# Turning normalised activations with 16-bit DMA transposes instead of TensorE, with the order of all stages written anew

## The chip, the cores and the metric

The kernel runs on one core of a Trainium2 chip. The metric is the device time of one execution in microseconds (us), and the time of a kernel is the median of its runs. One execution is also profiled; spans, waits and durations below come from that one.

## What is computed

Two graph layers run one after the other on 128 graphs of 128 nodes with 256 features, in fp32. The adjacency entries are 0 or 1. Cut to what matters:

```python
# layer 0: attention with one value matrix per adjacency value, then a feed-forward net
q, k = src @ Wq + bq, src @ Wk + bk                       # 8 heads of 32
attn = softmax(q k^T / sqrt(32))
out  = sum over r of (attn * (adj == r)) @ (src @ Wv[r] + bv[r])
x = LN(src + out @ Wo + bo) * g1 + beta1                  # norm 0
y = LN(x + gelu(x @ W1 + b1) @ W2 + b2) * g2 + beta2      # norm 1
# layer 1: two graph-attention steps, then a feed-forward net
h = gat(gat(y, adj, W1, a1), adj, W2, a2)                 # softmax over axis 1, masked by adj
z = LN(y + h) * g_ln1 + b_ln1                             # norm 2
out = LN(z + relu(z @ w_ff1 + b_ff1) @ w_ff2 + b_ff2) * g_ln2 + b_ln2   # norm 3
```

LN subtracts the mean of a row of 256 and divides by the root of its variance plus 1e-5.

## The kernel before, in words

The 16384 tokens are worked in 32 groups of 512 (four graphs, `G = 4`, `T = 512`). A group has its tokens in two layouts. In token layout a tile is 128 tokens on partitions x 4 blocks x 256 features (`S["x"]`, the residual, normalised in place). In feature layout it is 128 features x 2 halves x 512 tokens (`yT`), which TensorE needs as an operand. `transposed` (L293 to L306) goes from the first to the second: eight TensorE transposes into two PSUM banks (L300), and two ScalarE activations (L303) that take the result out of PSUM and apply the norm's gain and offset, which are per-partition columns in that layout.

A norm i of a group goes through these steps. `added` or the end of `ffn` adds to `x` and takes row statistics with VectorE (`variances`, L320 and L322). `root` (L334, L335) makes 1/sqrt(var + eps), a VectorE instruction and a power on GpSimd. `normed` (L338 to L357) makes (x - mean) / std: for norms 0 to 2 four ScalarE activations (L349) with a small VectorE one ahead (L344), for norm 3 four VectorE ones (L354). `turned` calls `transposed` and, for norms 0 and 2, makes four sums and differences `yS` on VectorE (L389 to L392). `scaled` (L367) multiplies the token-layout tile by the gain and adds the offset, in two VectorE passes of two 128x512 instructions each; its result is the residual of what follows.

The matrix products of the feed-forward nets and of the q, k, v projections use a scheme with seven instead of eight half-size products, so that sums such as `yS` stand ahead of them and VectorE adds (L466, L470, L479 to L481, L503 to L524) behind. `ffn` (L394 to L528) is a generator with 22 steps: 14 of the first layer, each one product of two 128x256 matmul instructions (L411) into the PSUM banks `fa`, `fe` or `seeded`, with ScalarE copies `p7` (L456) and `p16` (L460) and activations (L435); and 8 of the second layer, seven of them with a product of eight 128x128 instructions (L420). An fp32 matmul shows as two in the trace. `first_ffn` is layer 0's net and `second_ffn` layer 1's. `projected` makes q, k and v (L641); `attention` makes scores (L709), exponentials (L717), masked copies (L727), sums and denominators (L744, L758), reciprocals (L775, L777), and the output projection (L793); `layer1` makes both graph-attention steps. In these `spread` sends a 2 KB row block to HBM and back, broadcast over partitions (L840, L841). Of exp and gelu each needs its own ScalarE function table, loaded by `table` (L537).

The engines run their instructions in the order in which the kernel issues them (`manual_schedule`); nothing rearranges them later. That order is written by hand: every stage is a generator that stops at `yield`, and `in_order` takes steps of several groups by turns. In the steady part, a pass of the loop over `g` works on the first net of group g+1, the graph layer and second net of g, the attention and projections of g+2 and g+3, and the last norm of g-1. All DMAs of the steady part are issued by SyncE (SP), in order: `entered` loads a group's xT, adj and x together, and `store` writes a finished group.

In code, the part that the change replaces first:

```python
for b in range(G):
    nc.tensor.transpose(
        pt[:, b * P : (b + 1) * P], y[:, b, c * P : (c + 1) * P], k.ident
    )
nc.scalar.activation(
    yT[:, c, :], pt, AF.Identity, bias=bc[:, c : c + 1], scale=gc[:, c : c + 1]
)
```

Of the kernel before, what the change touches and what calls it, by code (L numbers as in the profile page):

```python
# [11 lines left out]
I32 = mybir.dt.int32  # L12
AF = mybir.ActivationFunctionType
# [12 lines left out]
G = 4  # L26
# [4 lines left out]
class Weights:  # L31
# [16 lines left out]
    def col(self, name):  # L48
        v = self.a[name]
        t = self.tile([P, v.shape[0] // P], "c_" + name)  # L50
        with self.nc.allow_non_contiguous_dma(reason="a bias vector as columns"):
            self.queue.dma_start(t, v.rearrange("(c p) -> p c", p=P))
        return t
# [45 lines left out]

def over(r, n=G):  # L100
    return r[:, None, :].to_broadcast([P, n, r.shape[1]])
# [6 lines left out]
def fast_pass(ctx, tc, a, out):  # L108
# [17 lines left out]
    io = ctx.enter_context(tc.tile_pool(name="io", bufs=4))  # L126
# [29 lines left out]
    def entered(g):  # L156

        xt = load_xT(g)
        ad, xr = load_rest(g)
        return dict(xt=xt, ad=ad, x=xr, g=g, direct={NG - 1: 0, NG - 2: 1}.get(g, 2))  # L160
# [44 lines left out]
    b0 = k.tile([P, NCH], "b0")  # L205
# [11 lines left out]
    g1c, be1c = k.col("L0_gnn_g1"), k.col("L0_gnn_beta1")  # L217
    w1, b1 = forms("L0_gnn_W1"), k.col("L0_gnn_b1")
    g1r = k.row("L0_gnn_g1")
# [15 lines left out]
    g2c, be2c = k.col("L0_gnn_g2"), k.col("L0_gnn_beta2")  # L235
    g2r, be2r = k.row("L0_gnn_g2"), k.row("L0_gnn_beta2")
    u1, c1 = forms("L1_gnn_w_ff1"), k.col("L1_gnn_b_ff1")
    u2 = forms("L1_gnn_w_ff2")
    h1c, he1c = k.col("L1_gnn_g_ln1"), k.col("L1_gnn_b_ln1")
# [9 lines left out]
    wu = k.tile([P, NCH, NU], "wu")  # L249

# [43 lines left out]
    def transposed(y, gc, bc, n):  # L294

        yT = w2p.tile([P, NCH, T], F32, tag="yT", name="yT_" + n)
        for c in range(NCH):
            pt = ps_s.tile([P, T], F32, tag="s", name=f"pt_{n}_{c}")
            for b in range(G):
                nc.tensor.transpose(  # L300
                    pt[:, b * P : (b + 1) * P], y[:, b, c * P : (c + 1) * P], k.ident
                )
            nc.scalar.activation(  # L303
                yT[:, c, :], pt, AF.Identity, bias=bc[:, c : c + 1], scale=gc[:, c : c + 1]
            )
        return yT  # L306

# [3 lines left out]
    def variances(S, i, bs):  # L311
# [9 lines left out]
        for b in range(bs.start, bs.stop):  # L321
            nc.vector.bn_aggr(S["mv", i][:, b, :], st[:, b % 2, :])  # L322

    def added(S, i, p, po):

        x = flat(S["x"][:, pair(p), :])
        nc.vector.tensor_add(x, po, x)
        variances(S, i, pair(p))

    def root(S, i, bs=slice(0, G)):  # L330

        n = f"{i}_{S['g']}_{bs.start}"
# [4 lines left out]
    def normed(S, i, bs=slice(0, G)):  # L337


        x, mv, rs = S["x"], S["mv", i], S["rs", i]  # L340
        scalar = i < 3 or bs.stop - bs.start < G
        if scalar:
            sh = small.tile([P, G], F32, tag="sh", name=f"sh_{i}_{S['g']}_{bs.start}")
            nc.vector.scalar_tensor_tensor(  # L344
                sh[:, bs], mv[:, bs, 0], -1.0, rs[:, bs], op0=ALU.mult, op1=ALU.mult
            )
        for b in range(bs.start, bs.stop):
            if scalar:
                nc.scalar.activation(  # L349
                    x[:, b, :], x[:, b, :], AF.Identity, bias=sh[:, b : b + 1],  # L350
                    scale=rs[:, b : b + 1],
                )
            else:
                nc.vector.tensor_scalar(  # L354
                    x[:, b, :], x[:, b, :], mv[:, b, 0:1], rs[:, b : b + 1],
                    op0=ALU.subtract, op1=ALU.mult,
                )  # L357
# [3 lines left out]
    cols = {0: (g1c, be1c), 1: (g2c, be2c), 2: (h1c, he1c)}  # L361

    def scaled(S, i, step, ps=range(G // 2)):
        for p in ps:
            x = S["x"][:, pair(p)]
            op = (nc.vector.tensor_mul, nc.vector.tensor_add)[step]
            op(x, x, over(rows[i][step], 2))  # L367

    def norm(S, i):

        root(S, i)
        yield
        normed(S, i)
        yield
        for step in range(2):
            scaled(S, i, step)
            yield

    TH = T // 2

    def turned(S, i):
        n = f"{i}_{S['g']}"
        S["xT", i + 1] = yT = transposed(S["x"], *cols[i], n)
# [8 lines left out]
        nc.vector.tensor_sub(ys[:, 3], a12, ys[:, 1])  # L392

    def ffn(S, i, wa, ba, func, wb_):  # L394
# [91 lines left out]
        def quarter(q, k2):  # L486

            return x[:, pair(q), k2 * P : (k2 + 1) * P]
# [52 lines left out]
    def in_order(*steps):  # L541


        for s in steps:
            if callable(s):
                s()
                continue
            gen, n = s if isinstance(s, tuple) else (s, 1)
            for _ in range(n):
                next(gen, None)  # L550

    def prepared(S):
        g, xr, ad = S["g"], S["x"], S["ad"]
        for p in range(G // 2):
            nc.vector.tensor_add(xr[:, pair(p)], xr[:, pair(p)], over(bo, 2))

# [6 lines left out]
    def projections(S):  # L563

# [9 lines left out]
        for h, (o, bias) in enumerate((("qT", bq), ("kT", bk))):  # L574
            S[o] = w1p.tile([P, NCH, T], F32, tag=o, name=f"{o}_{n}")
            for m in range(NCH):
# [6 lines left out]
                nc.scalar.activation(S[o][:, m, :], pq, AF.Identity, bias=bias[:, m : m + 1])  # L583
                yield
        S["v"] = v = w1p.tile([P, G, 2 * D], F32, tag="v", name="v_" + n)
        for b in range(G):
# [8 lines left out]
            nc.vector.tensor_add(v[:, b, D:], pv[:, D:], bv)  # L595
            yield
# [3 lines left out]
    def projected(S):  # L600
# [15 lines left out]
        S["qT"], S["kT"] = qk  # L616
        S["v"] = v = w1p.tile([P, G, 2 * D], F32, tag="v", name="v_" + n)

        for values in range(2):
# [26 lines left out]
            def result(k2, h):  # L646

                if values:
# [44 lines left out]
    def scores(S, p):  # L693

        qT, kT = S["qT"], S["kT"]
# [36 lines left out]
    def sums(S, p):  # L732


        e, pm = S["e", p], S["pm", p]
# [174 lines left out]
    def store(S, bs=slice(0, G)):  # L910
        t0 = S["g"] * T
# [27 lines left out]
    with tc.manual_schedule(engines={ET.PE, ET.Activation, ET.DVE, ET.SP, ET.Pool}):  # L939
# [4 lines left out]
        none = iter(())  # L944
        st = [first, second] + [None] * (NG - 2)
        S1 = st[1]
        gwu, pr, at = graph_weights(), projections(first), attention(first)
        pr1, at1 = projections(S1), attention(S1)
        n0, n1_, n0_ = norm(first, 0), norm(first, 1), norm(S1, 0)

        def output_bias():
# [7 lines left out]
            prepared(first)  # L959

        in_order(
            (pr, 4), (at, 3), (pr, 2), (at, 5), (pr, 2), at, output_bias, pr1, (at, 3), pr1, at, n0, (pr1, 3), (at1, 2), n0,
            lambda: combined(w1), pr1, at1, lambda: turned(first, 0), (at1, 4),
        )
        f1 = first_ffn(first)
        prepared(S1)
        st[2] = entered(2)
        pr = projected(st[2])
        in_order(
            gelu, (f1, 2), at1, at1, pr1, pr1, (f1, 4), at1, f1, f1, n0, lambda: combined(w2), f1,  # L970
            f1, n0, f1,
            (f1, 3), gwu, at1, f1, gwu, f1, at1, gwu,
            f1, at1, f1, gwu, lambda: combined(wqk), at1, f1, n0_, pr, n0_, (f1, 4), n1_, (pr, 5), lambda: turned(S1, 0),
        )
        for g in range(NG - 1):
            S, S1 = st[g], st[g + 1]
            more = g + 2 < NG
            f1, f2 = first_ffn(S1), second_ffn(S)
            n1, n2 = norm(S1, 1), norm(S, 2)
            at = n0 = none  # L980
            if more:
                S2 = st[g + 2]
                at, n0 = attention(S2), norm(S2, 0)
            ahead = lambda: turned(S, 2)
# [399 lines left out]
```

## Time and profile before

| | |
|---|---|
| runs | 2741.42, 2742.82, 2742.77 us; median 2742.77 |
| span of the profiled execution | 2740.1 us |
| TensorE busy | 2705.4 us (99%), 21621 matmuls |
| VectorE busy | 2282.8 us (83%) |
| ScalarE busy | 1610.6 us (59%) |
| GpSimd busy | 135.6 us (5%) |
| DMA | 86.12 MB, mean 31 GB/s |

The profiled execution's own time is not listed apart from its span; the median lies 2.7 us above that span, and what lies around the span is taken from this. PE in the profile is TensorE's matmuls, PEld its weight loads, DVE is VectorE, ACT ScalarE, POOL GpSimd, SP SyncE. A group's row gives the line, engine, operation, the tiles out and in, their shapes and the count; then its busy time in us, the mean ns of one, and how long the engine stood idle just before, with what ended that wait. The matmuls overlap one another: their mean duration is longer than the distance from one's start to the next one's, and that distance is what one costs in a full queue. The same holds, less strongly, for DVE and ACT. The granted TensorE clock is 1.00 in all windows read but the last 20 us.

### The profile page before, as it was taken

To read this page: it belongs to the slowest core of one execution; us is meant where nothing else is said; L and a number is where in the kernel's file an instruction comes from. 1 tells how busy PE (TensorE), PEld (TensorE's weight loads), DVE (VectorE), ACT (ScalarE), POOL (GpSimd) and SP (SyncE) were. 2 spreads that over 40 slices of the span, in tenths; PEclk is the share of its full clock that TensorE was granted. 3 is DMA by queue.
4 is the path that set the end of the run, shared out by engine and by line. 5 is a ranking of instruction groups with operands and counts; after the bars stand their busy time and mean duration, and the time that the engine had idled before them with its cause. 6 is when DMAs were issued, how large, how long until landed. Compare 5 with 4: busy or idle time off the path is not lost. (4 is left out here: it accounts for less than half of the span.)

```text
span 2740.1 us, 54262 instructions
## 1 busy us (share of the span) xinstructions
PE 2705.4 (99%) x21621; PEld 2374.2 (87%) x21621; DVE 2282.8 (83%) x5320; ACT 1610.6 (59%) x3587; POOL 135.6 (5%) x137
## 2 busy tenths in 40 slices
PE   9999999999999999999999999999999999999997
PEld 5888888888898888888888988888888889888876
DVE  5888888888888888888888888888888888888877
ACT  4555656556656556565566565565655665655654
POOL 0000000000000000000000000000000000000000
PEclk9999999999999999999999999999999999999999
DMA  6001110011100011100111000101001010001000
GB/s 179 1 24 36 32 36 16 25 35 33 35 21 31 24 36 32 36 17 24 36 32 36 20 32 24 36 32 36 17 24 36 32 36 18 34 24 36 13 13 17
DMA packets 70234, 86.12 MB, mean 31 GB/s; under 512 B 8428, under 2 KB 48728, under 8 KB 69976
## 3 DMA queue, kind: packets, MB, share of 16 engines
q1 hardware_dynamic: 68872, 82.20, 9.5%
q8 instruction: 172, 2.82, 0.4%
q14 instruction: 86, 0.70, 0.1%
q10 hardware_dynamic: 1104, 0.40, 0.1%
HBM read 65.68 MB, written 16.90 MB: 30 GB/s over the span
## 5 line engine op out<-in xcount | busy, mean ns | idle before, releaser
L349 ACT ACTIVATE x<-x,sh,rs 128x256 f32<-128x256 f32 x388 | 203.3, 609 | 425.8 <-DVE sh L344 425.8
L335 POOL TENSOR_TENSOR rs<-rs,mhalf 128x4 f32<-128x4 f32 x129 | 133.5, 1035 | 2553.5 <-DVE rs L334 2307.0
L411 PE MATMUL seeded<-yS,w_L_gnn_w_ff 128*128 128x256 f32 x768 | 207.2, 392 | 1.6 <-ACT seeded L483 1.6
L466 DVE TENSOR_TENSOR hT<-seeded,p 128x512 f32<-128x512 f32 x128 | 88.5, 692 | 140.9 <-ACT hT L435 83.5
L411 PE MATMUL seeded<-yS,w_L_gnn_W 128*128 128x256 f32 x768 | 201.2, 384 | 2.3 <-ACT seeded L483 1.3
L411 PE MATMUL ph<-yT,w_L_gnn_w_ff 128*128 128x256 f32 x768 | 202.7, 387 | 0.4 <-ACT yT L303 0.4
L320 DVE BATCH_NORM_STATS2 st<-x 128x6 f32<-128x256 f32 x512 | 192.2, 417 | 6.7
L411 PE MATMUL ph<-yT,w_L_gnn_W 128*128 128x256 f32 x768 | 197.4, 379 | 0.4 <-ACT yT L303 0.4
L411 PEld LDWEIGHTS seeded<-yS,w_L_gnn_w_ff 128*128 128x128 f32 x768 | 137.8, 189 | 66.3 <-issue 25.1
L420 PEld LDWEIGHTS po<-w_L_gnn_W,hT 128*128 128x128 f32 x1536 | 186.3, 192 | 4.8
L420 PE MATMUL po<-w_L_gnn_w_ff,hT 128*128 128x128 f32 x1536 | 187.0, 275 | 0.0
L420 PE MATMUL po<-w_L_gnn_W,hT 128*128 128x128 f32 x1536 | 187.0, 275 | 0.0
L420 PEld LDWEIGHTS po<-w_L_gnn_w_ff,hT 128*128 128x128 f32 x1536 | 184.1, 192 | 3.3
L411 PEld LDWEIGHTS seeded<-yS,w_L_gnn_W 128*128 128x128 f32 x768 | 138.0, 190 | 31.5 <-ACT p L460 2.2
L727 DVE TENSOR_TENSOR pm<-e,adj 128x512 f32<-128x512 f32 x256 | 159.2, 684 | 5.7 <-ACT e L717 5.7
L411 PEld LDWEIGHTS ph<-yT,w_L_gnn_W 128*128 128x128 f32 x768 | 145.6, 190 | 20.7 <-ACT yT L303 0.7
L411 PEld LDWEIGHTS ph<-yT,w_L_gnn_w_ff 128*128 128x128 f32 x768 | 140.7, 190 | 22.8 <-ACT yT L303 0.7
L717 ACT ACTIVATE e<-ps 128x512 f32<-128x512 f32 x256 | 134.2, 593 | 6.2 <-PE ps L709 4.0
L435 ACT ACTIVATE hT<-hT,c_L_gnn_b 128x256 f32<-128x256 f32 x256 | 109.6, 500 | 45.0 <-DVE hT L466 44.9
L849 ACT ACTIVATE gs<-spread,wh 128x128 f32<-128x128 f32 x120 | 38.5, 392 | 154.1 <-DMA spread<-hbm 154.1
L435 ACT ACTIVATE hT<-hT,c_L_gnn_b_ff 128x256 f32<-128x256 f32 x256 | 110.8, 524 | 30.9 <-DVE hT L466 29.2
L420 PEld LDWEIGHTS seeded<-w_L_gnn_W,hT 128*128 128x128 f32 x1024 | 124.3, 192 | 3.5 <-DVE hT L517 0.3
(195 smaller groups left out, 6494.4 us busy)
## 6 DMA issues: line engine op xcount, KB each, us to landing
xT<-in_xT_dram SPq DMA_DIRECT2D x32, 512.0 KB, 5.9
x<-in_x_dram SPq DMA_DIRECT2D x32, 512.0 KB, 5.2
out_dram<-x SPq DMA_DIRECT2D x31, 512.0 KB, 2.9
spread<-hbm SPq DMA_DIRECT2D x59, 256.0 KB, 3.1
adj<-in_adjT_dram SPq DMA_DIRECT2D x32, 256.0 KB, 4.0
w_L_gnn_W<-in_L_gnn_W_dram SPq DMA_DIRECT2D x8, 256.0 KB, 6.1
w_L_gnn_w_ff<-in_L_gnn_w_ff_dram SPq DMA_DIRECT2D x8, 256.0 KB, 4.9
hbm<-line SPq DMA_DIRECT2D x59, 2.0 KB
```

The source lines that it names most:

```text
L320: nc.vector.bn_stats(st[:, b % 2, :], S["x"][:, b, :])
L335: nc.gpsimd.tensor_tensor(rs[:, bs], rs[:, bs], k.mhalf[:, bs], op=ALU.pow)
L349: nc.scalar.activation(x[:, b, :], x[:, b, :], AF.Identity, bias=sh[:, b : b + 1], scale=rs[:, b : b + 1],)
L411: nc.tensor.matmul(bank[:, s * TH : (s + 1) * TH], wa[:, form, 0, f * P : (f + 1) * P], m, start=start and s == 0, stop=True, skip_group_c ...
L420: nc.tensor.matmul(bank[:, s * P : (s + 1) * P], m[:, f, s * P : (s + 1) * P], wb_[:, form, f, :], start=start and s + f == 0, stop=True, ...
L435: nc.scalar.activation(o[:, s], o[:, s] if src is None else src[:, s * TH : (s + 1) * TH], func, bias=ba[:, f : f + 1],)
L466: nc.vector.tensor_add(hidden(1, 1, r), halves(seeded), halves(p7))
L717: nc.scalar.activation(e[:, s], pss[s], AF.Exp, scale=SCALE)
L727: nc.vector.tensor_mul(pm[:, s], S["e", p][:, s], S["ad"][:, pair(p), None, :].to_broadcast([P, 2, NCH, P]),)
L849: nc.scalar.activation(s[:, b, :], target[:, b, :], AF.Identity, bias=source[:, b, :])
```

## The change

The change has three parts.

First, each of the norms 0 to 2 is finished in token layout, gain and offset with it, before it is turned. `affine` takes the place of `normed` and `scaled`: for each block of 128 tokens two VectorE instructions with three inputs, (x - mean) * gain and then x * (1/std) + offset. Norm 3 uses it too. The offset that is added contains the second bias of the feed-forward net that follows, since the same tile is its residual. What goes into the net is then too large by that bias, and `without` takes the bias's product with the first weights out of the net's first bias, once, with 16 matmuls of one column for each net.

Second, the turn is made by DMA. `sent` splits two blocks into 16-bit planes with two ScalarE copies (low and high halves of each fp32 word), and SyncE issues one DMA that transposes the 128 x 1024 two-byte tile. `turned` puts the planes together again with two ScalarE copies for each half of the group. The planes use the buffers of other tiles (`p7`, `p16`, `spread`, `gs`); the turned planes `pT` have two buffers.

Third, the order of all stages is written as three strings. In them a letter is a stage (`q` projections, `a` attention, `f` first net, `l` graph layer, `k` second net, `n0` to `n3` the norms, `t0` to `t2` the turns, `z` the last norm), then the group counted from the string's base, then the number of steps. FRONT is played once, STEADY 29 times, TAIL once. xT is loaded by `in`; adj and x by `rest`, for all but the first three groups, at another place. The residual tile has three buffers instead of four. Loads of the gain and offset columns go; loads of the two second biases as columns come.

```diff
-    io = ctx.enter_context(tc.tile_pool(name="io", bufs=4))
+    io = ctx.enter_context(tc.tile_pool(name="io", bufs=3))
...
-        xt = load_xT(g)
-        ad, xr = load_rest(g)
-        return dict(xt=xt, ad=ad, x=xr, g=g, direct={NG - 1: 0, NG - 2: 1}.get(g, 2))
+        S = dict(xt=load_xT(g), g=g, direct={NG - 1: 0, NG - 2: 1}.get(g, 2))
+        if g < 3:
+            S["ad"], S["x"] = load_rest(g)
+        return S
+
+    def rest(S):
+
+        S["ad"], S["x"] = load_rest(S["g"])
...
+    def without(b, w, col):
+
+        pb = mm_tile("pbias")
+        for f in range(NF):
+            h, m = divmod(f, NF // 2)
+            for c in range(NCH):
+                nc.tensor.matmul(
+                    pb[:, f : f + 1], w[:, PLAIN[c][h], 0, m * P : (m + 1) * P],
+                    col[:, c : c + 1], start=(c == 0), stop=(c == NCH - 1),
+                )
+        nc.vector.tensor_sub(b, b, pb[:, :NF])
...
-    def normed(S, i, bs=slice(0, G)):
+    def affine(S, i, bs=slice(0, G)):
...
+        for first in (True, False):
+            for b in range(bs.start, bs.stop):
+                nc.vector.scalar_tensor_tensor(
+                    x[:, b, :], x[:, b, :], mv[:, b, 0:1] if first else rs[:, b : b + 1],
+                    g if first else be, op0=ALU.subtract if first else ALU.mult,
+                    op1=ALU.mult if first else ALU.add,
+                )
+
+    def sent(S, i, p):
+
+        n = f"{i}_{S['g']}_{p}"
+        tag = (("p7", "p16"), ("spread", "gs"), ("spread", "gs"))[i][p]
+        planes = w1p.tile([P, 2, 2, D], U16, tag=tag, name="planes_" + n)
+        S["pT", i, p] = pT = w2p.tile([P, 2 * 2 * NCH, P], U16, tag="pT", name="pT_" + n)
+        for b in range(2):
+            words = S["x"][:, 2 * p + b, :].bitcast(U16).rearrange("p (k h) -> p h k", h=2)
+            nc.scalar.copy(planes[:, :, b], words)
+        nc.sync.dma_start(pT, planes.rearrange("p h b d -> p (h b d)"), transpose=True)
...
     def norm(S, i):

         root(S, i)
         yield
-        normed(S, i)
-        yield
-        for step in range(2):
-            scaled(S, i, step)
-            yield
+        for p in range(G // 2):
+            affine(S, i, pair(p))
+            yield
+            if i < 3:
+                sent(S, i, p)
+                yield
...
     def turned(S, i):
         n = f"{i}_{S['g']}"
-        S["xT", i + 1] = yT = transposed(S["x"], *cols[i], n)
+        yT = w2p.tile([P, NCH, T], F32, tag="yT", name="yT_" + n)
+        for p in range(G // 2):
+            pT = S["pT", i, p].rearrange("p (h b c) t -> p h b c t", h=2, b=2)
+            for c in range(NCH):
+                o = yT[:, c, p * D : (p + 1) * D].bitcast(U16)
+                nc.scalar.copy(
+                    o.rearrange("p (b t h) -> p h b t", b=2, h=2), pT[:, :, :, c, :]
+                )
+            if p == 0:
+                yield
+        S["xT", i + 1] = yT
+        yield
...
+STEADY = """
+l:0 t0:1 q:2 t0:1*2 q:2 f:1 q:2*2 f:1 q:2 l:0 k:-1 f:1 q:2*2 f:1*2 n3:-1 f:1 l:0 gelu q:2*2 f:1
+l:0 n3:-1 f:1 l:0 n3:-1 q:2*3 f:1*5 q:2*2 f:1 l:0*2 f:1 l:0 out:-1 f:1 a:2 l:0 rest:2 f:1 q:2
+a:2*2 q:2*3 l:0 q:2*2 n2:0 q:2*2 n2:0*3 f:1*2 q:2*2 n2:0 f:1 q:2*2 f:1 exp t2:0 in:3 q:2*2 t2:0
+f:1 n1:1 a:2*2 t2:0 k:0*3 a:2 n1:1 k:0 a:2 n1:1*3 a:2 k:0*2 a:2 k:0*3 t1:1 a:2 k:0 bo:2 t1:1 a:2
+l:1 k:0*2 a:2 l:1 k:0 l:1 a:2*2 n0:2 k:0 n0:2 k:0 l:1 n0:2 k:0 n0:2 k:0 l:1 k:0*4 q:3 n0:2
+"""
...
+        in_order(FRONT, 0)
+        for g in range(1, NG - 2):
+            in_order(STEADY, g)
+        in_order(TAIL, NG - 2)
```

In the built program the change takes 768 transposes off TensorE and adds 32 one-column matmul instructions there; ScalarE has 768 copies of 128x512 two-byte elements more and 580 activations fewer; SyncE has 192 transposing DMAs more. The ScalarE table loads now stand before the first gelu or exp that needs them, since the steps `gelu` and `exp` come after it in the order.

## The prediction

> **What bounds the kernel now.** I read the page's first part, then the busy times of the middle of the run, the timelines of TensorE and VectorE over one group of 512 tokens, the groups by form, and the DMA table.
>
> ```profile
> span 2740.1 us, 54262 instructions
> ...
> PE 2705.4 (99%) x21621; PEld 2374.2 (87%) x21621; DVE 2282.8 (83%) x5320; ACT 1610.6 (59%) x3587; POOL 135.6 (5%) x137
> ```
> ```profile
> 140.00:2640.00 2500.00, 2494.60 (x20091) 2203.48 (x20090) 2116.12 (x4917) 1493.50 (x3334) 124.42 (x120) 1.00 0.09 29
> ```
> In the window the columns after the length are PE, weight loads, DVE, ACT, POOL. TensorE is idle for 5.4 of 2500 us; VectorE is busy 85%. Outside it, PE is idle about 12 us in the first 140 and 17 in the last 100 (shorter windows). So TensorE is the bound, and its work counts one to one, until another engine binds over a stretch shorter than a group.
>
> ```profile
> 1000.11 1.04 PE L300 MATMUL pt<-ident,x 128*128 128x128 f32 x8
> 1000.99 1.12 PE L411 MATMUL ph<-yT,w_L_gnn_w_ff 128*128 128x256 f32 x4
> ...
> 1058.39 1.03 PE L641 MATMUL pvqa<-w_v,xT 128*128 128x256 f32 x4
> ...
> 1083.88 1.04 PE L300 MATMUL pt<-ident,x 128*128 128x128 f32 x8
> 1084.76 1.12 PE L411 MATMUL ph<-yT,w_L_gnn_w_ff 128*128 128x256 f32 x4
> ...
> 1087.77 0.40 PE L758 MATMUL pav<-pm,v 128*32 128x128 f32 x8
> ```
> The same step comes again after 1083.88 - 1000.11 = 83.77 us: a group's period. Eight transposes take 0.88 us from their start to the next step's.
>
> ```profile
> 1045.79 1.38 DVE L354 TENSOR_SCALAR x<-x,c_out,rs 128x256 f32<-128x256 f32 x4
> ...
> 1062.80 2.49 DVE L727 TENSOR_TENSOR pm<-e,adj 128x512 f32<-128x512 f32 x4
> 1065.20 0.68 DVE L327 TENSOR_TENSOR x<-pg,x 128x512 f32<-128x512 f32 x1
> ...
> 1079.62 1.74 DVE L777 RECIPROCAL rd<-rd 128x256 f32<-128x256 f32 x1
> ...
> 1083.29 0.69 DVE L466 TENSOR_TENSOR hT<-seeded,p 128x512 f32<-128x512 f32 x1 [1.33 <-PE seeded L411]
> ```
> VectorE runs here without a hole for some 20 us, and only then waits for PE (1.33 us). What it costs in a queue is start to start: four masks 2.40, a 128x256 pass 0.335 (L354: four in 1.29 to the next), a reciprocal 1.67.
>
> ```profile
> L349 ACT ACTIVATE x<-x,sh,rs 128x256 f32<-128x256 f32 x388 | 203.3, 609 | 425.8 <-DVE sh L344 425.8
> ...
> L300 PE MATMUL pt<-ident,x 128*128 128x128 f32 x768 | 102.6, 274 | 2.9 <-ACT x L349 2.3 <-DVE v L595 0.4
> ...
> L367 DVE TENSOR_TENSOR x<-x,r_L_gnn_g_ln 128x512 f32<-128x512 f32 x128 | 82.0, 679 | 0.5 <-ACTq L1350 0.5
> ...
> L460 ACT COPY p<-seeded 128x512 f32<-128x512 f32 x128 | 76.0, 594 | 16.9 <-PE seeded L411 16.9
> ```
> Behind the bar stand a group's busy time and the ns of one: what goes (L349, L300, one of four L367 groups) and the nearest row to what comes (L460).
> ```profile
> out_dram<-x SPq DMA_DIRECT2D x31, 512.0 KB, 2.9
> spread<-hbm SPq DMA_DIRECT2D x59, 256.0 KB, 3.1
> adj<-in_adjT_dram SPq DMA_DIRECT2D x32, 256.0 KB, 4.0
> ```
> The last number is us from issue to landing.
>
> **What the Trainium skill says.** "VectorE: DVE Perf Modes", section on the three transpose paths, gives 1309 ns for one 128x128 two-byte DMA transpose; this trace has no DMA transpose. "Advanced Engine Details and Errata", section X-Bar Transpose (TRN2), expects 350 to 400 GB/s of them. "DMA: Bandwidth & Descriptors", section on the anatomy of one DMA, gives about 2.0 us of fixed cost (for DMAs that GpSimd issues) plus the bytes; the trace's 512 KB store, 2.9 us, is of that order. "TensorE: Matmul & The Clock Gate", Part 4, sees about 275 ns for a TensorE transpose in a kernel; the trace agrees (274), but they overlap, and one costs 0.11 us.
>
> **The change, part by part.**
>
> *TensorE transposes go.* 3 norms x 32 groups x 8 = 768, at 0.11 us: 84.5 us, or 2.63 a group. Neither the 102.6 of the row nor 768 x 274 ns: both count tails under the next matmul. A group becomes 83.77 - 2.63 = 81.14.
>
> *Two bias corrections* add 32 matmuls of one column, 64 passes, about 0.11 each, at the front: 7 us; PE's holes there hide between nothing and all of it. I take 5.
>
> *ScalarE.* Gone: L349's 203.3 and L303's 93.9 + 46.3 = 343.5 us. New: 768 copies of 512 two-byte elements. The nearest row is L460, 594 ns, or 0.5 in a queue: 384 to 456. ACT ends near 63 to 65%. Two-byte strides are not in the trace; twice the price would put it near 80%. ACT holds in the steady part while a DMA lands, and behind it are attention's row sums and the FFN's copies, counted below. The table loads keep their number (65 to 67) but move to the first real gelu and exp; a load is 1.28 us. The gelu one has two products until PE needs the bank; the exp one lies in the edge step just ahead of the stretch below, with some tenths to spare. I take none, at most 1.28 a group.
>
> *VectorE.* Gone: scaled (L367) 328.9, L354 42.7, sh 13.2 = 385. New: 1024 passes of 128x256 at 0.335 to 0.416: 343 to 426. In sum nothing; but they sit elsewhere. In the program built from the changed file (its order is known, its times are not), look at DVE from L551, which waits for the first FFN's second-layer product T2, to the last mask of head pair 1, on which PE's next attention sums wait. With the start-to-start costs of the timeline: masks 2 x 2.40; 16 passes of norms 2 and 1 at 0.335, 5.36; two reciprocals 3.33; two GAT adds with statistics 3.30; five FFN output adds 1.80 and their statistics 1.88; two hT subtractions 1.20; five value adds 2.98; yS 1.48; roots 0.16; oT 0.61; hT adds 1.40. Sum 28.3. With 0.2 from PE's end to L551, 0.2 for a value product that comes late, and 0.1 at the end: 28.8. PE has exactly the same steps today between 1058.39 and 1087.77; less the transposes (0.97 + 0.88) that is 27.5. So DVE, not PE, sets this stretch, by 1.3 us a group; 30 groups: 40. Ends: nothing, if PE's small gaps and DVE's overlap are kinder; 1.3 + 16 x 0.08 = 2.6 a group if a pass costs 0.416. The rest of the group leaves DVE 43 us of work for 54 of PE; no second stretch is so tight.
>
> *DMA transposes.* 192 of 256 KB, six a group, on SP's queue. From below: about 2 + 0.66 = 2.7 us (an estimate from the skill's fixed cost and 400 GB/s); as estimates from above: 8 blocks x 1.309 = 10.5. The trace's nearest transfers of 256 KB land in 3.1 and 4.0. I take 3.5. How much is hidden: in the sum above, norm 2's second half leaves DVE after 10.0 us; its planes take 1.0 on ACT, the two copies behind the landing 1.0, and DVE comes to yS, which reads them, at 16.6. A landing up to 16.6 - 12.0 = 4.6 costs nothing; each further us delays DVE by one. Norm 1's first half has 4.6 + 1.3 by PE's steps until ScalarE's row sums queue behind its copy; norm 0 has some 6. So 3.5 costs nothing.
>
> *SP's queue and moved loads.* adj and x are now issued behind the store. x waits for that store (2.9), since there are three buffers instead of four, and lands 5.2 later; it is used 32 us of PE work after its step. adj (4.0) has about 5 us ahead of the masks. The spread pair (3.1) lies ahead of norm 0's transposes in the queue, which have time. Nothing on POOL moves ahead of its root; POOL is 5% busy.
>
> *Front and tail.* At the tail less work stands beside the transposes: 2 norms with a landing partly bare, some 4 us; storing the last halves separately may give 1 or 2 back. I take +4, ends -5 to +10.
>
> Sum: 2740.1 - 84.5 + 5 + 40 + 4 = 2704.6. The median, 2742.77, is 2.7 above the span: 2707, I say 2708.
>
> **Rivals.**
> A. *TensorE binds throughout*: DVE's stretch is no longer than PE's. For it: the stretch is a difference of 5% between two sums. Against: the queue today is closed already. 2708 - 40 = 2668.
> C. *The passes cost 0.416*, or the exp load pushes L551: another 1.25 us a group, 37 us: 2745, no change. Against: L354 and the statistics run at 0.335.
> B, slower. *The transposes land late.* Place: norm 2's yS on DVE, then norm 1's copy on ACT. What is left of a group's gain after DVE's 1.3 is 1.3, less 0.3 for the fixed 9 us: from a landing of about 4.6 + 1.0 = 5.6 us the kernel is slower. At 7 us: 2.4 at norm 2 and 1.1 at norm 1, 3.5 x 30 = 105: 2813. For it: 1309 ns for a single block, if blocks add up. Against: the bandwidths given.
> *That it doesn't do what it says* has no room: the built program has no transposes on PE and 192 on SP.
>
> **How the numbers follow.** Forecast 0.50 (its own range 2688 to 2730), A 0.20, C 0.14, B 0.16. The range runs from just under A to C: 2664 to 2745; B lies outside, and a little of A. A measurement tells 0.2% (5.5 us) from no change. Faster: forecast, A and a fifth of C, 0.73; same: half of C and a rim, 0.07; slower: B and the rest of C, 0.20.
>
> **What would show it.** No L300 group; PE's period 82.4 us; DVE's passes at 0.335 start to start; a PE wait of 1 to 2 us a group on the hT add or the mask of the attention sums, named DVE. A period of 81.1 says A. A median landing over 5.6 us with yS waiting for ACT or ACT for DMA says B. DVE busy about 2280 to 2320, ACT about 1650 to 1730. I am wrong if two-byte copies on ACT cost far over 0.6 us, or if a wait appears where I left none, as at the exp load.

## The result, and the profile after

The changed kernel takes 2732.74 us (median of 6 runs, 2728.58 to 2735.18), beside 2742.64 for the kernel before in the same rounds: ratio 0.9961, 95% interval 0.995 to 0.9972, so 0.39% faster. The forecast was 2708 us, 1.27% faster. The profiled execution took 2731.53 us; its span is 2729.7, 10.4 less than before.

The first part of the page with the rows of the two new ScalarE copies and of the DMA transposes, then the middle of the run (columns as before: PE, weight loads, DVE, ACT, POOL):

```profile
span 2729.7 us, 53540 instructions
...
PE 2664.3 (98%) x20917; PEld 2308.5 (85%) x20917; DVE 2322.0 (85%) x5612; ACT 1750.6 (64%) x3777; POOL 142.3 (5%) x137
...
L393 ACT COPY planes<-x 128x512 uint16<-128x512 uint16 x384 | 216.5, 629 | 216.6 <-DVE x L379 216.6
L419 ACT COPY yT<-pT 128x512 uint16<-128x512 uint16 x384 | 267.3, 769 | 94.1 <-DMA pT<-planes 93.2
...
pT<-planes SPq DMA_TRANSPOSE x192, 3.1
```
```profile
140.00:2640.00 2500.00, 2466.59 (x19556) 2148.72 (x19557) 2171.42 (x5242) 1642.33 (x3550) 131.29 (x120) 1.00 0.20 48
```
The transposes are gone from TensorE; its idle time in the window went from 5.4 to 33.4 us.

**One group.** TensorE's timeline over one group (start, duration, then the operation; in brackets what it waited for):

```profile
1318.61 1.89 PE L945 MATMUL pg<-yh,gs 128*128 128x256 f32 x8
...
1331.12 1.03 PE L680 MATMUL pvqa<-w_v,xS 128*128 128x256 f32 x4
1332.08 0.43 PE L800 MATMUL pav<-e,v 128*32 128x128 f32 x8
1333.12 0.43 PE L800 MATMUL pav<-pm,v 128*32 128x128 f32 x8 [0.61 <-DVE v L695]
...
1334.67 1.04 PE L786 MATMUL pden<-e,ones 128*32 128x512 f32 x8
...
1346.26 0.30 PE L800 MATMUL pav<-pm,v 128*32 128x128 f32 x1 [0.20 <-DVE pm L768]
...
1401.32 1.89 PE L945 MATMUL pg<-yh,gs 128*128 128x256 f32 x8
```
The same step comes again after 1401.32 - 1318.61 = 82.71 us. The period was 83.76, forecast 82.4, and TensorE's work alone was to give 81.14. The two waits stand at the attention sums (`pav`, L800), for VectorE each time: the first sums of a group wait for the last addition of values, the second ones for the masks. Adding up start to next start, each of these two steps took 1.77 us before; now the first takes 2.59 and the second 2.53. So practically the whole 1.57 between 81.14 and 82.71 lies there (1.58). The brackets show less, 0.61 and 0.20: idle time counts from the end of the matmul before, and each of these is listed with 0.27 us, while in a full queue the next one starts at most some 0.11 us after it. The kernel before had the last value product at the same place, but followed by eight transposes:

```profile
1072.45 1.03 PE L641 MATMUL pvqa<-w_v,xS 128*128 128x256 f32 x4
1073.31 1.04 PE L300 MATMUL pt<-ident,x 128*128 128x128 f32 x8
1074.28 0.42 PE L758 MATMUL pav<-e,v 128*32 128x128 f32 x8
...
1076.05 1.04 PE L744 MATMUL pden<-e,ones 128*32 128x512 f32 x8
```
Their 0.97 us covered VectorE's addition of the values (L655, 1073.63 to 1074.31). With the transposes gone, that addition stands bare.

VectorE in the same group, from L551 to the masks of head pair 1:

```profile
1317.19 0.42 DVE L551 TENSOR_TENSOR x<-seeded,x 128x256 f32<-128x256 f32 x1
1317.52 2.48 DVE L768 TENSOR_TENSOR pm<-e,adj 128x512 f32<-128x512 f32 x4
...
1325.29 0.88 DVE L379 SCALAR_TENSOR_TENSOR x<-x,rs,r_L_gnn_b_ln 128x256 f32<-128x256 f32 x2
1326.09 0.88 DVE L379 SCALAR_TENSOR_TENSOR x<-x,mv,r_L_gnn_g_ln 128x256 f32<-128x256 f32 x2
1326.88 0.88 DVE L379 SCALAR_TENSOR_TENSOR x<-x,rs,r_L_gnn_b_ln 128x256 f32<-128x256 f32 x2
...
1332.38 0.68 DVE L695 TENSOR_TENSOR v<-pvqa,bv 128x512 f32<-128x512 f32 x1
...
1343.72 2.49 DVE L768 TENSOR_TENSOR pm<-e,adj 128x512 f32<-128x512 f32 x4
1346.12 0.69 DVE L522 TENSOR_TENSOR h<-hT 128x512 f32<-128x512 f32 x1
```
No line of this stretch waits for anything. Two passes take 0.79 us start to start, 0.396 each; the forecast had 0.335. From L551 to the end of these masks it is 1346.12 - 1317.19 = 28.93 us; the forecast's sum was 28.3.

**The front.** The start of a group's `pg` product (L903 before, L945 after) is a ruler for the whole run. Groups 1 and 29, before and after:

```profile
225.13 1.89 PE L903 MATMUL pg<-yh,gs 128*128 128x256 f32 x8
...
2570.52 1.89 PE L903 MATMUL pg<-yh,gs 128*128 128x256 f32 x8
```
```profile
242.42 1.89 PE L945 MATMUL pg<-yh,gs 128*128 128x256 f32 x8
...
2560.00 1.89 PE L945 MATMUL pg<-yh,gs 128*128 128x256 f32 x8
```
At group 1, 17.3 us are lost. From there to group 29, 27.8 us are won over 28 groups. From there to the end of the span it is 169.6 and 169.7: the tail is even. 17.3 - 27.8 + 0.1 = -10.4. So most of the gain was lost ahead of the steady groups. The timeline of the first such loss:

```profile
40.94 0.69 ACT L619 ACTIVATE kT<-pq,c_L_gnn_bk 128x512 f32<-128x512 f32 x1 [1.03 <-PE pq L615]
...
45.61 0.72 POOL L72 TENSOR_TENSOR r_L_gnn_b_ln<-r_L_gnn_b_ln,temp 128x256 f32<-128x256 f32 x1 [22.72 <-DMA temp<-in_L_gnn_b_ff_dram]
46.29 1.02 POOL L368 TENSOR_TENSOR rs<-rs,mhalf 128x4 f32<-128x4 f32 x1
47.35 0.88 DVE L379 SCALAR_TENSOR_TENSOR x<-x,rs,r_L_gnn_beta 128x256 f32<-128x256 f32 x2 [7.16 <-POOL rs L368]
47.86 1.14 ACT L393 COPY planes<-x 128x512 uint16<-128x512 uint16 x2 [6.24 <-DVE x L379]
...
48.91 0.68 ACT L619 ACTIVATE kT<-pq,c_L_gnn_bk 128x512 f32<-128x512 f32 x1
...
49.64 2.09 PE L750 MATMUL ps<-qT,kT 32*128 32x128 f32 x30 [6.61 <-ACT kT L619]
```
Read it upwards. TensorE's scores wait 6.61 us for the second half of kT. That copy stands on ScalarE behind norm 0's plane copies of group 0, which wait for VectorE's second pass, which waits for GpSimd's root, which stands behind an addition of two bias rows (L72) that waits for a row to land. Before, the same addition held the root too, but kT's copy lay ahead of everything that needs the root:

```profile
43.64 0.69 ACT L583 ACTIVATE kT<-pq,c_L_gnn_bk 128x512 f32<-128x512 f32 x1 [1.03 <-PE pq L579]
43.93 0.73 POOL L70 TENSOR_TENSOR r_L_gnn_b_ln<-r_L_gnn_b_ln,temp 128x256 f32<-128x256 f32 x1 [20.96 <-DMA temp<-in_L_gnn_b_ff_dram]
44.62 1.02 POOL L335 TENSOR_TENSOR rs<-rs,mhalf 128x4 f32<-128x4 f32 x1
...
49.17 2.08 ACT L349 ACTIVATE x<-x,sh,rs 128x256 f32<-128x256 f32 x4
```
After the hole comes a second loss. Busy times in short stretches of the changed kernel; the third number from the end is the granted clock:

```profile
50.00:54.00 4.00, 3.64 (x39) 3.35 (x36) 0.00 (x0) 2.57 (x6) 0.00 (x0) 0.50 0.37 70
54.00:58.00 4.00, 4.00 (x20) 4.00 (x20) 0.00 (x0) 0.52 (x2) 0.00 (x0) 0.50 0.55 93
58.00:62.00 4.00, 4.00 (x13) 3.43 (x13) 2.58 (x5) 0.00 (x0) 0.00 (x0) 0.50 0.84 302
...
118.00:122.00 4.00, 4.00 (x18) 3.73 (x19) 2.44 (x5) 4.00 (x10) 0.00 (x0) 0.55 0.73 135
```
Before, the clock is 1.00 in all of these. Here it is halved for some 17 us from 47 on, a stretch in which the first bias correction also runs (52.1 to 58.9), and for 7 us from 118 on, where TensorE had no hole but had begun the second bias correction 2 us earlier.

### The profile page after: what moved, and what is told of

Read it like the earlier page. It is cut to its first block, busy times and chain, and to the rows that moved or that the text cites. A ratio compares the mean times of both kernels' runs of the same rounds, so it can differ in the third digit from the quotient of the medians.

```text
span 2729.7 us, 53540 instructions
## 1 busy us (share of the span) xinstructions
PE 2664.3 (98%) x20917; PEld 2308.5 (85%) x20917; DVE 2322.0 (85%) x5612; ACT 1750.6 (64%) x3777; POOL 142.3 (5%) x137
## 4 chain that ended last, share of the span: by engine, by line
PE 53%; DVE 34%; ACT 8%; issue 3%; DMA 1%; SPq 1%; POOL 0%; ACTq 0%; DVEq 0%; POOLq 0%
PE ph L454 9%; PE seeded L454 9%; PE po L463 9%; DVE x L379 6%; PE seeded L463 6%; DVE pm L768 4%; PE pw L919 4%; PE pwo L835 4%; DVE st L350 3%; ACT hT L478 3%; PE pqqa L680 3%; PE pqqb L680 3%; PE pav L800 2%; PE py L932 2%; DVE rd L817 2%
## 5 line engine op out<-in xcount | busy, mean ns | idle before, releaser
L393 ACT COPY planes<-x 128x512 uint16<-128x512 uint16 x384 | 216.5, 629 | 216.6 <-DVE x L379 216.6
L419 ACT COPY yT<-pT 128x512 uint16<-128x512 uint16 x384 | 267.3, 769 | 94.1 <-DMA pT<-planes 93.2
L368 POOL TENSOR_TENSOR rs<-rs,mhalf 128x4 f32<-128x4 f32 x129 | 140.1, 1086 | 2535.9 <-DVE rs L367 2535.9
L509 DVE TENSOR_TENSOR hT<-seeded,p 128x512 f32<-128x512 f32 x128 | 88.1, 688 | 139.2 <-PE seeded L454 139.1
L454 PE MATMUL ph<-yT,w_L_gnn_w_ff 128*128 128x256 f32 x768 | 195.4, 383 | 0.8 <-ACT hT L478 0.8
L800 PE MATMUL pav<-pm,v 128*32 128x128 f32 x2048 | 126.0, 275 | 25.1 <-DVE v L695 19.2
L463 PE MATMUL seeded<-w_L_gnn_W,hT 128*128 128x128 f32 x1024 | 130.6, 279 | 1.0 <-DVE hT L561 1.0
```

What stands on the lines that cost most here:

```text
L368: nc.gpsimd.tensor_tensor(rs[:, bs], rs[:, bs], k.mhalf[:, bs], op=ALU.pow)
L393: nc.scalar.copy(planes[:, :, b], words)
L419: nc.scalar.copy(o.rearrange("p (b t h) -> p h b t", b=2, h=2), pT[:, :, :, c, :])
L454: nc.tensor.matmul(bank[:, s * TH : (s + 1) * TH], wa[:, form, 0, f * P : (f + 1) * P], m, start=start and s == 0, stop=True, skip_group_c ...
L463: nc.tensor.matmul(bank[:, s * P : (s + 1) * P], m[:, f, s * P : (s + 1) * P], wb_[:, form, f, :], start=start and s + f == 0, stop=True, ...
L800: nc.tensor.matmul(pav[s * DH : (s + 1) * DH, u, c, :], v[:, d0 : d0 + DH], m[:, s, u, c, :], start=(r == 0), stop=(r == 1),)
```

## The experiments

Periods and group starts are read from the `pg` starts as above; the period is the one that most groups show. The kernel before took 2742.2 to 2743.1 us beside these runs, so a difference of 1 us between two experiments of different rounds says nothing.

**E1: one instruction on GpSimd moved.** The row addition is put behind the first root:

```
-    he1c2 = k.row_sum("L1_gnn_b_ln1", "L1_gnn_b_ff2", cut(D))
+    he1c2, c2r = k.row("L1_gnn_b_ln1"), k.row("L1_gnn_b_ff2", t=cut(D))
...
+            he=lambda: nc.gpsimd.tensor_add(he1c2, he1c2, c2r),
...
-... a:0*2 n0:0 q:1*2 n0:0*2 ...
+... a:0*2 n0:0 he q:1*2 n0:0*2 ...
```


> One instruction is moved: GpSimd's addition of the two bias rows of layer 1 (it waits for the last of the bias rows to land) is put behind the first root of group 0 in GpSimd's queue, instead of ahead of it. Theory front: that addition holds the root, the root holds VectorE's second pass, that holds ScalarE's plane copy, and behind the copy in ScalarE's queue stands the copy of kT for which TensorE's scores wait 6.6 us; the clock is then granted at 0.50 for some 14 us. If so the hole is gone, the clock stays at 1.00 from 50 to 62 us, and 10 to 13 us go: 2720 to 2723. Rival: the front is set by the weights that are still landing, and the next wait takes the hole's place: no more than 3 us go, 2730 to 2733. Group period unchanged at 82.7 in both.

Measured: 2722.33 us, ratio 0.9924 (0.9911 to 0.9938). The hole went:

```profile
39.62 1.19 POOL L368 TENSOR_TENSOR rs<-rs,mhalf 128x4 f32<-128x4 f32 x1 [16.30 <-DVE rs L367]
...
43.53 1.17 PE L750 MATMUL ps<-qT,kT 32*128 32x128 f32 x30 [0.36 <-ACT kT L619]
```
10.4 us for one instruction: theory front holds. The period stays 82.71. One part of the expectation failed: the clock still falls to 0.50 from 47 to 54 us, now without a hole, 2 us after the first bias correction begins (45.3).

**E2: the order on ScalarE instead.** The addition stays; norm 0's passes and copies go behind kT's copy and the exponentials:

```
-n0:0 q:1*2 n0:0*2 q:1 a:1*2 n0:0*2
+n0:0 q:1*3 a:1*2 n0:0*4
```


> Only the order of the front is changed: norm 0's passes and plane copies of group 0 come behind group 1's copy of kT and its exponentials in the queues, and GpSimd's addition stays ahead of the root. Theory front: the same 6.6 us hole goes, because what reached TensorE came by ScalarE's queue; again 10 to 13 us less than the changed kernel, about 2720 to 2723. Rival (what reaches TensorE came by VectorE's masks or by a landing): a hole of 3 us or more stays before 60 us, and the time is 2726 or more.

Measured: 2722.39 us in one run; group 1's `pg` starts at 233.75, in E1 at 232.07. The same gain from the other end of the chain: the wait reached TensorE by ScalarE's queue.

**E3: no DMA transposes.** The plane copies write `pT` itself:

```
+        planes = pT.rearrange("p (h b c) t -> p h b (c t)", h=2, b=2)
...
-        nc.sync.dma_start(pT, planes.rearrange("p h b d -> p (h b d)"), transpose=True)
```


> Leaves out the 192 DMA transposes: ScalarE's plane copies write the tile that the DMA filled, all other instructions stay (the values are not turned). Theory: landings of 3.1 us cost nothing in the steady groups; the period stays within 0.1 us of 82.7. Only the front's waits for a landing (3.85 us at 209 us, and the slow clock after it) and the tail's go: 4 to 9 us less, 2724 to 2729. Rival (landings delay yS on VectorE or a copy on ScalarE, which sets the period): the period falls by 0.5 or more, and the time to 2715 or less.

Measured: 2731.2 us, ratio 0.996 (0.9944 to 0.9975); period 82.71. Landings cost the steady groups next to nothing: from group 1 to 29 it is 2316.4 us against 2317.6. The guess on the front was wrong, and with it the time of 2724 to 2729: the hole near 209 us stays without any landing.

```profile
210.95 1.51 PE L453 MATMUL ph<-yT,w_L_gnn_W 128*128 128x256 f32 x4 [3.84 <-ACT yT L418]
```

**E4: half of the passes of norms 1 and 2 left out.**

```
-        for first in (True, False):
+        for first in (True,) if i in (1, 2) else (True, False):
```


> Leaves out the second pass (times root, plus beta) of norms 1 and 2: 8 of a group's 16 vector passes in VectorE's stretch, 3.2 us. Theory stretch: VectorE's queue from the first FFN's product T2 to the masks of head pair 1 sets the period, TensorE waits 1.57 us a group for it; with 3.2 us less the waits for the value addition and for the masks go, and the period is TensorE's own 81.14, at most 81.3: about 42 us less than the changed kernel, 2688 to 2692. Rival (the exponential's table load, or TensorE's own gaps, make the 1.57): the period is 82.2 or more, and the time 2715 or more.

Measured: 2710.56 us, ratio 0.988 (0.9865 to 0.9896); period 82.11, between the two forecasts. With 3.2 us less on VectorE a group wins only 0.60: the second sums, which wait for the masks, fell from 2.53 to 2.12 us (1.77 before the change), the first, which wait for the value addition, from 2.59 to 2.41. Its bracket is still 0.43:

```profile
1487.29 0.43 PE L800 MATMUL pav<-pm,v 128*32 128x128 f32 x8 [0.43 <-DVE v L695]
```
So the first wait is for the most part not a late VectorE, but the way from the product over the addition and back. Of the second about half stays as well: VectorE now waits 0.53 us for a product of TensorE ahead of the two hT additions (L509, L513) and the masks.

**E5: the last value product earlier.** The last value product and its addition come before the first net's last two second-layer products, which then stand between it and the sums; norm 2's second half goes behind one value addition. Nothing is left out:

```
-q:2*2 n2:0*3 f:1*2 q:2*2 n2:0 f:1 q:2*2 f:1 exp t2:0 in:3 q:2*2 t2:0
+q:2*2 n2:0*2 f:1 q:2*2 n2:0 f:1 q:2*2 n2:0 q:2*2 f:1*2 exp t2:0 in:3 t2:0
```


> Order only: in every middle group the last value product and its addition come before the first FFN's last two second-layer products, and the second half of norm 2's passes behind the first-taken addition of the values; VectorE's work is the same. Theory last addition: 0.6 of TensorE's 1.57 us a group is nothing but the way of the last value product over VectorE's addition back to the attention sums, which stood bare once the transposes were gone from this place; period 82.1, total 16 to 18 us below the changed kernel, about 2714. Rival, theory stretch: VectorE's queue is closed up to the masks of pair 1, so the wait for the value addition only moves to the masks or to yS: period 82.5 or more, total at most 6 us less, 2726 or more.

Measured: 2739.11 us, ratio 0.9985 (0.9978 to 0.9992): 6 us slower than the change. Period 82.83, and in four groups 84.1; in three of these ScalarE waits 2.9 us for a landing.

```profile
1428.43 1.13 PE L454 MATMUL seeded<-yS,w_L_gnn_w_ff 128*128 128x256 f32 x4 [0.97 <-DVE hT L509]
...
1431.43 0.30 PE L800 MATMUL pav<-pm,v 128*32 128x128 f32 x1 [0.20 <-DVE pm L768]
```
The value wait is gone (first sums 1.77 us, as before the change) and has come back as a wait for the hT addition; the second sums stay at 2.53. The rival held.

**E6: a quarter of the stretch's passes on GpSimd** (norm 1, second pair):

```
+        if (i, bs.start) == (1, 2):
+            for b in range(bs.start, bs.stop):
+                nc.gpsimd.tensor_scalar(x[:, b, :], x[:, b, :], mv[:, b, 0:1], rs[:, b : b + 1],
+                    op0=ALU.subtract, op1=ALU.mult)
+            for r, op in ((g, ALU.mult), (be, ALU.add)):
+                nc.gpsimd.tensor_tensor(x[:, bs], x[:, bs], over(r, 2), op=op)
+            return
```


> Norm 1's passes of the second pair of blocks (4 of VectorE's 16 in the stretch, 1.6 us) are done by GpSimd in four instructions, from the numbers of its addition of 128x256 in the front (0.72 us) some 4 us. Theory stretch: the masks of pair 1 come 1.6 us earlier, the waits for the hT addition and the masks (0.2 and the broken sums) go, the wait for the value addition, which lies ahead, stays: period 82.2 to 82.3, total 12 to 15 us less, about 2717. Rival (GpSimd and VectorE slow each other down, or the later plane copies hold ScalarE's queue): VectorE's passes beside it take over 0.45 us each or TensorE waits for ScalarE; period 82.7 or more, total 2731 or more.

Measured: 2731.57 us, ratio 0.9957 (0.994 to 0.9974): hardly a gain in all, for the front lost 2.3 us more (group 1 at 244.74 against 242.42) and the tail 3.4. Period 82.48: the second sums fell to 2.12 us, as in E4, and the first stayed at 2.59. GpSimd took 5.7 us for the four instructions; the estimate was 4.

**E7: turning back on TensorE**, all else as changed (passes on VectorE, new orders, bias corrections); `sent` does nothing:

```
-            pT = S["pT", i, p].rearrange("p (h b c) t -> p h b c t", h=2, b=2)
+            pt = mm_tile(f"pt_{n}_{p}")
             for c in range(NCH):
...
+                    nc.tensor.transpose(
+                        pt[:, (2 * c + b) * P : (2 * c + b + 1) * P],
+                        S["x"][:, 2 * p + b, c * P : (c + 1) * P], k.ident)
+            nc.scalar.copy(yT[:, :, p * D : (p + 1) * D], pt.rearrange("p (c t) -> p c t", c=NCH))
```


> One part undone: the turning goes back to TensorE (8 transposes a norm and two copies of 128x512 by ScalarE), without planes and DMA transposes; the norm on VectorE and all orders stay as changed. Theory stretch: the transposes add 2.63 us of TensorE work a group, of which what lies in the stretch (norm 2's 0.88) is hidden by waits that TensorE has there anyway: period 84.4 to 84.7, total 50 to 60 us above the changed kernel, 2781 to 2792. Rival additive: every transpose counts and the waits stay: 85.3, total 2810. Rival (the transposes never cost 2.63 and the DMA way brings no more than the 1.05 that the period fell): 83.8, total 2763 or less.

Measured: 2778.07 us, ratio 1.0126 (1.0109 to 1.0143). One group of it:

```profile
1419.83:1504.34 84.51, 84.51 (x675) 74.00 (x674) 72.29 (x175) 43.39 (x100) 4.37 (x4) 1.00 0.10 29
```
Period 84.51, as theory stretch said (the total is 3 us below its range): the transposes fill most of what were waits, and the sums take 1.97 and 2.09 us instead of 2.59 and 2.53. This run splits the change, counted in this order: all the rest (passes, orders, bias corrections) costs 2778.1 - 2742.6 = 35.5 us with the turn on TensorE, and turning by DMA instead then brings 2778.1 - 2732.7 = 45.4, ScalarE's copies included.

**E8: the front spliced.** E1, and the last third of the front in the order of the middle groups:

```
-in:3 a:2*2 f:1 t2:0 n1:1 k:0 a:2 k:0*2 a:2 n1:1*4 a:2 k:0*3 t1:1*2 ... l:1 n0:2 k:0 n0:2*3 q:3 l:1 k:0*2 n0:2
+in:3 f:1 n1:1 a:2*2 t2:0 k:0*3 a:2 n1:1 k:0 a:2 n1:1*3 ... n0:2 k:0 l:1 n0:2 k:0 n0:2 k:0 l:1 k:0*4 q:3 n0:2
```


> The front with GpSimd's addition moved as in the first experiment, and its last third replaced by the order that the middle groups have there. Theory front: the 3.85 us hole at 209 us is an ordering of norm 0 of group 2 too close behind its output product (it stayed when no DMA was there), not a landing; with the middle groups' order it is under 1 us, and with it 1.4 us of halved clock: 4 to 8 us below the first experiment's 2722, about 2716. Rival (VectorE has more to do there than in a middle group, so the wait moves elsewhere): 2720 to 2726.

Measured: 2716.59 us, ratio 0.99 (0.9884 to 0.9917), as expected; group 1 at 227.97. No wait of TensorE near 209 us is left, so the second hole was an order too tight for norm 0.

**E9: no bias corrections** (E8 with `b1` and `c1` taken out of the front; the hidden biases stay uncorrected).

> The kernel of the spliced front (2716.6), with both bias corrections left out (the 64 one-column passes on TensorE and two subtractions; the hidden biases stay uncorrected). Theory clock: those passes take 6.0 and 4.3 us there, and the granted clock falls to 0.50 some 2 us after each begins and comes back some 5 us after its end, although TensorE has no hole then; without them the clock stays at 1.00 from 40 to 130 us, and 10.3 plus about 4.6 us of half clock go: about 2702. Rival hole: the clock falls because of the small waits around 42 to 46 us, and TensorE's time there is set by what it waits for: the clock still falls to 0.50 before 60 us, and 4 us at most go, 2712 or more.

Measured: 2710.67 us, ratio 0.9886 (0.987 to 0.9901). The clock stays 1.00 from 30 to 104 us, so those falls did come from the passes; but only 5.9 of the 15 us went (8.2 at group 1 in the profiled executions). Their time had covered other waits: where the second correction stood, TensorE now waits 3.1 us for a ScalarE copy (L700, until 104.7), and after that hole the clock falls to 0.50 for some 3 us. The size of theory clock was wrong.

**E10: bias corrections as wide passes** (E8 otherwise):

```
+                nc.tensor.matmul(
+                    pb, col[:, c : c + 1].to_broadcast([P, P]), w[:, PLAIN[c][h], 0, :],
+                    start=(c == 0), stop=(c == NCH - 1))
+            for m in range(NF // 2):
+                nc.vector.scalar_tensor_tensor(
+                    scr, pb[:, m * P : (m + 1) * P], 1.0, k.ident, op0=ALU.mult, op1=ALU.mult,
+                    accum_out=t[:, h * NF // 2 + m : h * NF // 2 + m + 1])
```


> The spliced front, with the bias corrections computed otherwise: the bias column, broadcast, is the loaded side and the weights stream, 4 passes of 512 columns in place of 32 of one, and VectorE picks the diagonal with 8 small passes (some 2.3 us a correction). Theory clock: 4 passes take some 1.8 us (an estimate from 0.43 us a pass of 128x512 in the front) and keep TensorE busy, so no fall of the clock: 2716.6 - 10.3 - 4.6 + 3.6 = 2705. Rival hole, or VectorE becomes late in the front: 2712 or more.

Measured: 2712.13 us, ratio 0.989 (0.9875 to 0.9905): 4.5 less than E8, on the edge of the rival. Around the second correction, E8 and then this kernel:

```profile
110.00:114.00 4.00, 4.00 (x18) 3.64 (x18) 2.19 (x5) 4.00 (x11) 0.00 (x0) 0.57 0.71 132
114.00:118.00 4.00, 4.00 (x12) 3.20 (x12) 1.29 (x2) 2.80 (x6) 0.00 (x0) 0.58 0.00 0
```
```profile
110.00:114.00 4.00, 4.00 (x18) 3.06 (x17) 3.65 (x16) 4.00 (x10) 0.00 (x0) 1.00 0.58 106
114.00:118.00 4.00, 4.00 (x20) 3.48 (x20) 2.64 (x9) 4.00 (x11) 0.00 (x0) 1.00 0.00 0
```
No fall there, nor at the first correction; so it was the row of one-column passes that lowered the clock. Two things took the rest of the gain. The four passes show as eight matmuls in the trace, since they are fp32, and took 3.5 and 3.4 us, not 1.8 each: 3.4 of the 7 us missed. And near 55 us a 1.9 us wait for a value addition came up, with 0.50 for some 3 us after it.

**E11: relu for gelu** (no table loads in the groups; the function of the first FFN is another).

> The changed kernel with relu in place of gelu in the first FFN, so that ScalarE loads no table in the groups. Theory load: the load ahead of the edge exponential makes VectorE's stretch begin 0.77 us late; without it the masks and the hT addition of pair 1 come so much earlier, TensorE's 0.2 there and part of the broken sums go, and the value wait (0.61) shrinks to some 0.45: period 82.2 to 82.4, total 2719 to 2723. Rival: what stands ahead in VectorE's queue hides the load, period 82.6 or more, total 2729 or more.

Measured: 2726.02 us, ratio 0.9944 (0.9929 to 0.9959); period 82.60. The loads cost 0.11 us a group: the rival is nearer, for without them VectorE waits for product T2 instead (0.63 us at L551 in one group).

**E12: all together.** E8, E10, E5's order, E6's passes from group 3 on; nothing is left out.

> All together, and nothing left out: spliced front, GpSimd's addition behind the root, wide bias corrections, last value product first (as in e5), and norm 1's second pair on GpSimd from group 3 on (as in e6). Theory stretch: alone, e5 moved its wait to the hT addition (0.97 us) and e6 left the value wait (0.61); together VectorE has the 1.6 us that e5's order needs, so both waits go: period 81.9 to 82.1, total 2705 - 28 x 0.7 = 2685, range 2680 to 2692. Rival: the later second half of norm 2 makes yS late whatever VectorE does, period 82.5 or more, 2700 or more.

Measured: 2690.81 us, ratio 0.9819 (0.9806 to 0.9832): the fastest, 1.5% below the change. Period 81.48, TensorE's own 81.14 plus 0.34. E5 alone lost 0.12 a group and E6 alone won 0.23; together they win 1.23. E5's order frees the first sums (1.77 us), and with E6's passes off VectorE the wait for the hT addition, in which E5 lost this again, does not come back. But the second wait is not gone, as was expected: the second sums still take 2.37 us. 0.98 of the 1.23 lie at the sums, the rest is spread over several products. That the total lies in the expected range is partly luck: most groups are shorter than the 81.9 to 82.1 expected, and longer ones bring the mean to 81.97. Four groups take 83.9 or 84.0: in the one from 1122.72 to 1206.68 ScalarE waits 2.96 us for a landing (1.14 in a usual group), and with it the row sums behind:

```profile
1138.52 1.39 ACT L434 COPY yT<-pT 128x512 uint16<-128x512 uint16 x2 [2.96 <-DMA pT<-planes]
...
1139.78 0.58 ACT L825 ACTIVATE rd<-pden 128x512 f32<-128x512 f32 x1
```
In this order a landing has no time to spare: what rival B said of a late landing does happen here, but hardly in the order of the change (E3).

## Why the prediction was right and wrong

The sum forecast -35.5 us of span against -10.4. Set against the `pg` starts: for the 28 middle groups it gives 28 x (1.33 - 2.64) = -36.7, measured -27.8; for all else 4 x -2.64 + 2 x 1.33 + 9 = +1.1, measured 17.3 + 0.1 = +17.4. Of the 25 us missed, 16 lie in the front and 9 in the groups.

- *Transposes, 2.63 a group*: right. TensorE's busy time in a group differs by 84.51 - 81.90 = 2.61 between E7 and the change.
- *"Front and tail ... I take +4, ends -5 to +10"*: **this step failed.** It looked at the tail, which is even, and gave the front no walk of its own; the front lost 17.3 us. *"Nothing on POOL moves ahead of its root"* was true and beside the point: the root had waited for a bias row before, too. What moved was ScalarE's kT copy, behind copies that need the root. E1 and E2, the two ends of that chain, each bring 10 us; putting the second order error right (E8) brings 4.1 more at group 1.
- *Two bias corrections, 5*: too small. The passes took 7.0 and 4.5 us and ran in part under a halved clock; doing them otherwise brings 4.5 (E10). What E1, E8 and E10 win at group 1, 10.4 + 4.1 + 3.6 us, makes 18.0, about the 17.3 lost.
- *VectorE's stretch, 1.3 a group*: the place and the sign right, the size 1.57 instead, and half of the reason missing. A pass costs 0.396, so the 16 have 1.0 more than the 0.335 gave. That price was read wrongly: L354's four passes in 1.29 are 0.323 each, and they read one tensor; 0.335 is a plain addition, and no row of before has the new form at this size. But 0.82 of the 1.57 stand at the value addition, whose cover were the very transposes that go, and 0.64 of that stay when VectorE has 3.2 us less to do (E4). I had put it down as "0.2 for a value product that comes late". Nor was the queue quite closed before: of the 20 us "without a hole", VectorE waited 0.5, 0.2 and 0.2 us (L389, L390, L775). What one wait costs depends on the other (E5, E6, E12).
- *Table loads, 0 to 1.28*: taken 0, measured 0.11 (E11).
- *DMA transposes, 3.5 us and free*: landed in 3.1, nearly free in the groups (E3: 1.2 us over 28 of them). Of the two estimates from the Trainium skill, the one from fixed cost and bandwidth (2.7) was near; the one that adds 1309 ns for each block (10.5) was not. The slack was thinner than thought once the order moved (E5, E12).
- *ScalarE*: 64% against 63 to 65. The copies cost 629 and 769 ns on average; two plane copies take 1.14 together and two back 1.39.
- *SP's queue and the moved loads, nothing*: no wait named them in the groups.

Rival A, 2668, would have needed both waits gone. No run shows that: E12 comes near, with a period of 81.48, but keeps 0.60 us at the second sums. With the transposes back on TensorE (E7) the new order still has a period of 84.51, not 83.76, though TensorE counts as busy all the time. Start to next start, the sums take 4.06 us there instead of 3.54 and the transposes 2.92 instead of 2.71, which together is nearly all of the 0.75: waits shorter than the listed length of a matmul do not show as idle time. What holds the transposes stays open.

## What to carry to other kernels

Work that is taken away may be somebody's cover: ask what runs on other engines beneath it, here one addition that the removed transposes hid. Where all orders are written anew, walk the first groups queue by queue as carefully as the steady one: an old, harmless wait (a bias row on GpSimd) becomes a hole when an instruction that TensorE needs is put behind it. And one wait relieved alone can bring nothing where two stand in a row (E5): try them together (E12).

## What the runs showed of the hardware

- Thirty-two passes of one column in a row bring the granted clock to 0.50 with TensorE never idle: in the second correction the passes went from 250 to 353 ns. With both corrections left out (E9) the clock stays at 1.00 until a hole near 103 us, and with wide passes (E10) it stays there through both corrections. The Trainium skill, "TensorE: Matmul & The Clock Gate", Part 1 (the HAM clock gate), has the clock set by recent activity and lowered after an idle window of some 3.4 us; the 6.6 us hole agrees with it (the clock falls 3.7 us after the hole begins). The passes show that a busy row of the profile is not activity enough, and shorter holes were followed by 0.50 too: 3.1 us in E9 and 1.9 us in E10. The same 1.9 us in E12 were not.
- A DMA transpose of 256 KB from SBUF to SBUF landed in 3.0 to 4.5 us, median 3.1, and cost SP's queue 1.23 us to issue.
- A VectorE pass that reads two tensors and a scalar for each row costs 0.396 us for 128x256, a plain addition 0.335, start to start in a queue.
- GpSimd needed 2.99 us for two passes of 128x256 with two operations each, and 1.27 for a plain one of 128x512 (E6).
